# A router's maximum subtracted on VectorE: a transformer block with two-of-four experts on one Trainium2 core

## The chip, the core and the metric

The kernel runs on one core of one Trainium2 chip. A core has five engines that run side by side, each with its own queue of instructions that it takes strictly in order: TensorE (PE; its weight loads are shown apart as PEld), VectorE (DVE), ScalarE (ACT), GpSimd (POOL) and SyncE (SP), which issues most of the transfers. An instruction starts when its engine has reached it and the semaphores that it waits for have been raised. SBUF is the on-chip memory, 128 partitions wide; PSUM is the memory that TensorE writes to. "128x8" means 128 partitions of eight columns.

The metric is the device time of one execution in microseconds (us). A profile is one further execution, recorded by the hardware; its span is the time from its first to its last instruction.

## What is computed

32 sequences of 256 tokens with 128 channels pass through one pre-norm block: attention with 16 heads of 8 channels, in which the softmax is replaced by a rational function of the score minus the row's maximum, and a feed-forward layer of four experts, of which each token uses the two with the highest probability:

```python
x = x + attn(layernorm(x), w_qkv, w_out, b_out)
x = x + ffn(layernorm(x), router_w, router_b, w1, w3, w2)

# ffn, for all tokens xf (t, d)
logits = xf @ router_w + router_b                    # (t, 4)
probs = softmax(logits, axis=-1)
top_p, top_i = top_k(probs, 2)
top_p = top_p / sum(top_p, axis=-1)
gates = zeros((t, 4)); gates[token, top_i] += top_p
h = silu(einsum('td,edf->etf', xf, w1)) * einsum('td,edf->etf', xf, w3)
out = einsum('te,etd->td', gates, einsum('etf,efd->etd', h, w2))
```

Everything is float32. The softmax's common divisor drops out of the gates: it is enough to take exp(logit - maximum), set the two smaller ones to zero and divide by the sum of the rest.

## The kernel before

One sequence is one *block* b, 0 to 31. A block's 256 tokens lie on the 128 partitions in two halves, so that a tile with one number per token is 128x2, and the router's logits (four per token) are 128x8. The work of a block is cut into some sixty kinds of *steps*, each a small Python function that issues a few instructions on one engine (`ENGINE`, L73, says which). A planner (`plan`, L274) lays the steps of all blocks out in one order, by hand-set ranks (`RANK`, `OVER`), assumed costs (`COST`) and the numbers of buffers (`LIMIT`); `tile_block` then issues them in that order, and each engine's queue holds its share of it. A step's rank, its dependencies and its cost in the plan do not change when the body of its function does. The blocks overlap deeply: while ScalarE works at the attention of one block, TensorE runs the experts of an earlier one.

The steps that matter here, with their lines and the names that the profile shows:

- **Router.** `r_df` (GpSimd, L868 to L882) makes the logits `lg` from the normalised tokens, and `df`, 128x32, which says for each pair of experts which comes first; its last instruction is L882. `r_cnt` (VectorE) takes the maximum over the four logits of a token, negated, into `nm` (L888), and counts in `cnt` how many experts come ahead of each (L889). `r_exp` (ScalarE) takes the exponential in place, through the helper `act` (all its instructions have line L569): once for each half of the tokens, because a bias is one number per partition. `r_gs` (GpSimd) turns `cnt` into a mask (L900) and multiplies the exponentials by it (L901); `r_sm` (VectorE) sums them and takes the reciprocal (L905, L906); `r_ga` (GpSimd, L912) scales.
- **Tables.** ScalarE's functions come in tables. `act` loads a table where the function needs another than the last one (L567): one that holds the logarithm and the exponential serves `r_exp` and the attention's `l_ln` and `l_exp`; silu needs another. So there are two loads a block, and in most blocks one of them stands right behind `r_exp`.
- **Attention.** TensorE writes scores into two PSUM buffers, `ps_sc` (`c_pe`, L699: one buffer for scores to be processed, one for scores of a later block of which only the extreme is sought). VectorE's `x_red` reads the second (L710, `mt<-ps_sc`); ScalarE's `m_sq` squares the first (`dt<-ps_sc,sqb`), VectorE's `m_poly` completes it (L754, `dt<-dt,ps_sc`). TensorE's next scores into a buffer wait for L710 or L754. `l_prod` (L762) and `l_back` (L782) on GpSimd and `l_ln`, `l_exp` on ScalarE make reciprocals; `av` multiplies by the values.
- **After it.** `p_evac` and `tr_copy` are ScalarE's copies out of PSUM (`otsb`, `rxnT`, `ronT`, `rxn2T`); `p_norm` on VectorE divides (L812 and L814, `rc` and `on`); `p_add` makes the second norm's statistics (L835 to L845); `split` on GpSimd cuts float32 into two parts (L508, L509; `q<-qr` for queries and keys, `hxnT`, `lxnT` for tokens). In the first two blocks some of these splits run on VectorE.
- **Experts.** `u_a` and `u_b` on TensorE (`ps_ab<-hxn2T,w1h` and the like), `u_silu` on ScalarE (`sl<-ps_ab`), `u_mul` on VectorE (L940, `ht<-sl,ps_ab`), `d_pe` on TensorE (`ps_ab<-w2s,ht`), `d_acc` on VectorE (L956).

The queue on VectorE holds, in nearly all blocks, L888, L889 and then the next `x_red` or `m_poly`. On GpSimd the split of the queries and keys (L508, L509) follows directly on `r_df` in blocks 4 to 25.

Of the kernel before, what the change touches and what calls it, by code (L numbers as in the profile page):

```python
# [10 lines left out]
F32 = mybir.dt.float32  # L11
F32R = mybir.dt.float32r
I32 = mybir.dt.int32
AF = mybir.ActivationFunctionType
ALU = mybir.AluOpType
AX = mybir.AxisListType
# [4 lines left out]
E, FF = 4, 512  # L21
P = 128
# [53 lines left out]
    DVE="x_red x_fin m_poly p_norm p_add r_cnt r_sm u_mul d_acc ln1_stats setup_wqk setup_const",  # L76
# [379 lines left out]
def tile_block(ctx: ExitStack, tc: tile.TileContext, x, wqk, wv, wo, bo, rw, rb, w1, w3, w2, out):  # L456
    nc = tc.nc
    NB = x.shape[0]
    PE, ACT, DVE, POOL, SP = nc.tensor, nc.scalar, nc.vector, nc.gpsimd, nc.sync
# [33 lines left out]
    p2 = ctx.enter_context(tc.tile_pool(name="p2", bufs=2))  # L493
# [8 lines left out]
    st = {}  # L502
# [61 lines left out]
    def act(o, i, f, **kw):  # L564
        need = SET_SILU if f == AF.Silu else SET_LNEXP if f in (AF.Ln, AF.Exp) else None
        if need and cur["set"] != need:
            ACT.preload_act_table_set(need)  # L567
            cur["set"] = need
        ACT.activation(o, i, f, **kw)  # L569
# [314 lines left out]

    def r_cnt(b):
        lg, df = st["rt", b]
        nm, cnt = p2.tile([P, 2], F32, tag="nm", name="nm"), p2.tile([P, 2, E], F32, tag="cnt", name="cnt")
        DVE.tensor_reduce(nm, lg, axis=AX.X, op=ALU.max, negate=True)  # L888
        DVE.tensor_reduce(cnt, df, axis=AX.X, op=ALU.add)  # L889
        st["cnt", b] = cnt, nm  # L890

    def r_exp(b):
        pr, (_, nm) = st["rt", b][0], st["cnt", b]
        for c in range(2):
            act(pr[:, c], pr[:, c], AF.Exp, bias=nm[:, c : c + 1])

    def r_gs(b):
        pr, _ = st["rt", b]
        cnt, _ = st.pop(("cnt", b))
        POOL.tensor_scalar(cnt, cnt, 2.0, 1.0, ALU.is_lt, ALU.mult)  # L900
        POOL.tensor_tensor(pr, pr, cnt, op=ALU.mult)  # L901

# [188 lines left out]
```

## Time and profile before

| | |
|---|---|
| time, median of 3 runs | 1104.97 us (1104.2 to 1105.72) |
| the profiled execution: time | 1104.63 us |
| its span, first to last instruction | 1102.7 us |
| granted TensorE clock, mean | 0.961 (1.00 from 236.48 to 871.90 us) |
| busy: PE, DVE, ACT, POOL | 1046.3, 949.4, 938.6, 780.6 us |
| the two exponentials `lg<-lg,nm`, 128x4 each | 64 instructions, mean 348 ns |
| L888 and L889 | 32 of each, mean 146 and 181 ns |
| table loads L567 | 64, 1283 ns each |

A timeline's row gives the start (us from the span's beginning), the length, engine, line, operation, names (written from read), shapes, and in brackets the engine's idle time before it with what ended that. Rows of one engine may overlap a little: an instruction that waits for nothing starts before the end of its forerunner has been recorded. The chain of waits is found by going back from the last instruction, at each step to what released it; its pieces are the stretches that the end of the program hangs on. Idle time of an engine off that chain costs nothing. Busy time is an average over stages and says little of what a change is worth; a weight load or matmul that is held up may also count as busy. "Releasers" are inferred from semaphores, and of several the last one is named.

### The profile page before, as it was taken

To read this page: it belongs to the slowest core of one execution; us is meant where nothing else is said; L and a number is where in the kernel's file an instruction comes from. 1 tells how busy PE (TensorE), PEld (TensorE's weight loads), DVE (VectorE), ACT (ScalarE), POOL (GpSimd) and SP (SyncE) were. 2 spreads that over 40 slices of the span, in tenths; PEclk is the share of its full clock that TensorE was granted. 3 is DMA by queue.
4 is the path that set the end of the run, shared out by engine and by line. 5 is a ranking of instruction groups with operands and counts; after the bars stand their busy time and mean duration, and the time that the engine had idled before them with its cause. 6 is when DMAs were issued, how large, how long until landed. Compare 5 with 4: busy or idle time off the path is not lost.

```text
span 1102.7 us, 25445 instructions
## 1 busy us (share of the span) xinstructions
PE 1046.3 (95%) x10025; PEld 867.5 (79%) x10025; DVE 949.4 (86%) x1662; ACT 938.6 (85%) x1157; POOL 780.6 (71%) x1063
## 2 busy tenths in 40 slices
PE   4578999999999999999999999999999999999988
PEld 3345787888888888888888888888888888888878
DVE  5777899899899998899999998899998889898644
ACT  2388888889988888999888889988888999888962
POOL 3457787687787787887877787877877887756320
PEclk7557999999999999999999999999999999999999
DMA  4722012221112222211122122122222211220000
GB/s 145 252 70 89 23 59 73 92 75 62 46 46 94 76 74 69 94 52 47 61 75 95 68 76 75 37 69 73 75 74 69 75 47 42 72 74 9 6 5 11
DMA packets 51791, 75.11 MB, mean 68 GB/s; under 512 B 5080, under 2 KB 41432, under 8 KB 47704
## 3 DMA queue, kind: packets, MB, share of 16 engines
q1 hardware_dynamic: 50664, 72.24, 19.4%
q8 instruction: 79, 1.29, 0.5%
q10 hardware_dynamic: 1008, 1.25, 0.3%
q14 instruction: 40, 0.33, 0.1%
HBM read 42.27 MB, written 31.20 MB: 67 GB/s over the span
## 4 chain that ended last, share of the span: by engine, by line
ACT 55%; PE 32%; DVE 5%; issue 3%; POOL 2%; DMA 2%; ACTq 0%; DVEq 0%
ACT dt L569 31%; PE ps_ab L505 27%; ACT prod L569 9%; ACT L567 6%; PE ps_sc L505 4%; ACT sl L569 4%; POOL dt L782 2%; DVE mt L710 2%; DVE dt L754 2%; DVE ht L940 1%; ACT qr L627 1%; ACT lg L569 1%; ACT rxnT L597 1%; ACT rxn2T L597 1%; ACT va L642 1%
## 5 line engine op out<-in xcount | busy, mean ns | idle before, releaser
L710 DVE TENSOR_REDUCE mt<-ps_sc 128x4 f32<-128x1024 f32 x256 | 310.8, 1217 | 37.1 <-PE ps_sc L505 36.8
L754 DVE SCALAR_TENSOR_TENSOR dt<-dt,ps_sc 128x1024 f32<-128x1024 f32 x256 | 310.3, 1213 | 18.7 <-ACT dt L569 13.5
L569 ACT ACTIVATE dt<-ps_sc,sqb 128x1024 f32<-128x1024 f32 x256 | 286.2, 1120 | 32.8 <-PE ps_sc L505 32.6
L782 POOL TENSOR_TENSOR dt<-dt,prod 128x2048 f32<-128x2048 f32 x59 | 271.4, 4603 | 14.5 <-ACT prod L569 14.1
L505 PE MATMUL ps_ab<-w2s,ht 128*128 128x128 f32 x2048 | 263.8, 278 | 1.1 <-DVE ht L940 1.1
L569 ACT ACTIVATE dt<-dt 128x2048 f32<-128x2048 f32 x138 | 260.7, 1920 | 0.2 <-DVE dt L754 0.2
L505 PEld LDWEIGHTS ps_ab<-w2s,ht 128*128 128x128 f32 x2048 | 242.7, 192 | 16.6 <-issue 9.9
L569 ACT ACTIVATE sl<-ps_ab 128x512 f32<-128x512 f32 x256 | 149.7, 597 | 74.6 <-PE ps_ab L505 63.2
L762 POOL TENSOR_TENSOR prod<-dt 128x1024 f32<-128x1024 f32 x59 | 141.2, 2394 | 90.1 <-DVE dt L754 90.0
L940 DVE TENSOR_TENSOR ht<-sl,ps_ab 128x512 f32<-128x512 f32 x256 | 169.0, 680 | 28.7 <-PE ps_ab L505 20.6
L505 PE MATMUL ps_sc<-qk 26*128 26x256 f32 (+1 forms) x2048 | 159.4, 346 | 20.4 <-DVE dt L754 9.7
L505 PE MATMUL ps_ab<-hxn2T,w1h 128*128 128x256 f32 x512 | 159.8, 312 | 4.4 <-DVE ht L940 1.4
L505 PEld LDWEIGHTS ps_sc<-qk 26*128 26x128 f32 (+1 forms) x2048 | 98.2, 193 | 72.8 <-issue 18.1
L505 PE MATMUL ps_ab<-hxn2T,w3h 128*128 128x256 f32 x512 | 153.9, 301 | 0.0
L505 PE MATMUL ps_ab<-hxn2T,w1l 128*128 128x256 f32 x512 | 144.3, 282 | 0.0
L505 PE MATMUL ps_ab<-lxn2T,w3h 128*128 128x256 f32 x512 | 144.2, 282 | 0.0
L505 PE MATMUL ps_ab<-lxn2T,w1h 128*128 128x256 f32 x512 | 144.1, 281 | 0.0
L505 PE MATMUL ps_ab<-hxn2T,w3l 128*128 128x256 f32 x512 | 144.1, 281 | 0.0
L505 PE MATMUL ps_ab<-dt,va 128*32 128x256 f32 x2048 | 137.4, 399 | 7.0 <-ACT dt L569 3.7
L569 ACT ACTIVATE prod<-prod 128x1024 f32<-128x1024 f32 x118 | 125.0, 1060 | 0.8 <-POOL prod L762 0.4
L505 PEld LDWEIGHTS ps_ab<-hxn2T,w1h 128*128 128x128 f32 x512 | 96.4, 188 | 24.0 <-ACT sl L569 8.8
L505 PEld LDWEIGHTS ps_ab<-hxn2T,w3h 128*128 128x128 f32 x512 | 96.6, 189 | 8.4 <-issue 1.6
(124 smaller groups left out, 1558.4 us busy)
## 6 DMA issues: line engine op xcount, KB each, us to landing
qk<-scr SPq DMA_DIRECT2D x31, 1024.0 KB
scr<-q SPq DMA_DIRECT2D x125, 128.0 KB
scr<-q SPq DMA_DIRECT2D x29, 256.0 KB
out_dram<-x SPq DMA_DIRECT2D x32, 128.0 KB
xg<-in_x_dram SPq DMA_DIRECT2D x7, 512.0 KB
ws<-in_w_dram SPq DMA_DIRECT2D x8, 256.0 KB
qk<-scr SPq DMA_DIRECT2D x2, 512.0 KB
mscr<-m SPq DMA_DIRECT2D x31, 32.0 KB
```

Source lines behind the costliest of these rows:

```text
L505: PE.matmul(o, l, r, start=start, stop=stop, skip_group_check=True)
L567: ACT.preload_act_table_set(need)
L569: ACT.activation(o, i, f, **kw)
L597: ACT.copy(raw, st.pop((i, b)))
L627: ACT.copy(qr, st.pop(("qkP", b)))
L642: ACT.copy(v36[:, :, :, 26 * r : 26 * r + HD], pv[:, :, :D].rearrange("p c (a r d) -> p c a r d", r=2, d=HD)[:, :, :, r])
L710: DVE.tensor_reduce(o, st.pop(("xP", b, t)), axis=AX.X, op=ALU.min, negate=True)
L754: DVE.scalar_tensor_tensor(d, d, C, st.pop(("mP", b, s)).rearrange("p j c s -> p (j c s)"), ALU.add, ALU.mult)
L762: POOL.tensor_tensor(pr, d[:, :, 0], d[:, :, 1], op=ALU.mult)
L782: POOL.tensor_tensor(d, d, pr[:, :, None, :].to_broadcast([P, 4, 2, S]), op=ALU.mult)
L940: DVE.tensor_tensor(ht, st.pop(("sl", b, s)), st.pop(("uP", b, s, 1)), op=ALU.mult)
```

## The change

The maximum is kept as it is instead of negated, VectorE subtracts it from the logits in place, and ScalarE takes one exponential of all eight columns without a bias. The order of the steps stays, so the subtract stands in VectorE's queue right behind the count (L889), and the exponential where the two were.

```diff
     def r_cnt(b):
         lg, df = st["rt", b]
-        nm, cnt = p2.tile([P, 2], F32, tag="nm", name="nm"), p2.tile([P, 2, E], F32, tag="cnt", name="cnt")
-        DVE.tensor_reduce(nm, lg, axis=AX.X, op=ALU.max, negate=True)
+        mx, cnt = p2.tile([P, 2], F32, tag="mx", name="mx"), p2.tile([P, 2, E], F32, tag="cnt", name="cnt")
+        DVE.tensor_reduce(mx, lg, axis=AX.X, op=ALU.max)
         DVE.tensor_reduce(cnt, df, axis=AX.X, op=ALU.add)
-        st["cnt", b] = cnt, nm
+        DVE.tensor_tensor(lg, lg, mx[:, :, None].to_broadcast([P, 2, E]), op=ALU.subtract)
+        st["cnt", b] = cnt
 
     def r_exp(b):
-        pr, (_, nm) = st["rt", b][0], st["cnt", b]
-        for c in range(2):
-            act(pr[:, c], pr[:, c], AF.Exp, bias=nm[:, c : c + 1])
+        pr = st["rt", b][0]
+        act(pr, pr, AF.Exp)
 
     def r_gs(b):
         pr, _ = st["rt", b]
-        cnt, _ = st.pop(("cnt", b))
+        cnt = st.pop(("cnt", b))
         POOL.tensor_scalar(cnt, cnt, 2.0, 1.0, ALU.is_lt, ALU.mult)
         POOL.tensor_tensor(pr, pr, cnt, op=ALU.mult)
```

In the instruction lists of the two programs VectorE has 32 instructions more, each behind L889 and waiting for VectorE's own L888; ScalarE has 32 activations less; the lists of TensorE and GpSimd are the same. The exponential waits, as before, for VectorE and GpSimd.

## The prediction, made before the changed kernel ran

> **What bounds the kernel now.** I read the chain of waits first, then engine timelines around one block of the even middle stretch (blocks 4 to 24 repeat every 31.76 us). The page's chain by engine:
>
> ```profile
> ACT 55%; PE 32%; DVE 5%; issue 3%; POOL 2%; DMA 2%; ACTq 0%; DVEq 0%
> ```
>
> The same chain in order of time (start, us, what), around the exponential of block 13:
>
> ```profile
> 521.69 0.45 ACT rxnT L597
> 522.14 0.38 ACT lg L569 x2
> ...
> 522.53 1.28 ACT L567
> 523.82 0.01 issue
> 523.83 0.61 ACT sl L569
> ...
> 524.48 3.83 PE ps_ab L505 x30
> ```
>
> ScalarE (ACT) is never idle from 533.28 of one block to 522.5 of the next; the two exponentials (`lg L569 x2`) stand in that run, before a table load (L567) and the first silu, whose end lets TensorE go on. From 524.48 TensorE has the chain until the last silu (533.88). So ScalarE time saved at the exponential counts in full, if no other path reaches 524.48 first.
>
> **What is removed.** Two ACTIVATEs of 128x4 with a bias per partition (64 in all, mean 348 ns) become one of 128x8 without. In the chain the old pair occupies 0.38 us; mid-stream they follow each other, and the next one them, by 0.188 each, again 0.376. The new one is not in the trace. From above: it behaves as one of the old, 0.19. From below: an eight-column copy (`xb L644`) takes 0.06 of the chain. Nearest are Exp without bias, from SBUF: 2048 columns 1.92 us, 1024 columns 1.06, so 0.84 ns a column; two in a row of 2048 take
>
> ```profile
> 513.46 3.73 ACT L569 ACTIVATE dt<-dt 128x2048 f32<-128x2048 f32 x2
> ```
>
> so the second adds 1.81, that is 0.09 beyond its columns (2048 x 0.84 = 1.72). I take 0.09 + 8 x 0.00084 = 0.10 for the new one: 0.38 - 0.10, rounded down, is **0.27 us a block** (bounds 0.19 to 0.32).
>
> Does 524.48 follow? Before it TensorE's last weight load of `ident,on` started 0.486 earlier; where it needn't wait (blocks 1 and 3) the next follows by 0.115, so 0.37 is free. VectorE (DVE) must start `ht` (L940) too; its row follows `sm L906` by 0.276, and rows that wait for nothing follow L906 by 0.083, so 0.19 is free there. It then runs back to back until its `dt L754` releases the scores that TensorE starts at 528.24: L754 ends 0.131 before, while in a case where TensorE really waited for L754 (539.78) it took 0.05, so 0.08 more is free. 0.19 + 0.08 = 0.27: the whole saving just fits. VectorE's rows (start, us):
>
> ```profile
> 519.97 0.13 DVE L888 TENSOR_REDUCE nm<-lg 128x2 f32<-128x8 f32 x1
> 520.01 0.17 DVE L889 TENSOR_REDUCE cnt<-df 128x8 f32<-128x32 f32 x1
> 520.11 1.21 DVE L710 TENSOR_REDUCE mt<-ps_sc 128x4 f32<-128x1024 f32 x1
> 521.42 1.22 DVE L754 SCALAR_TENSOR_TENSOR dt<-dt,ps_sc 128x1024 f32<-128x1024 f32 x1
> 522.89 0.36 DVE L812 RECIPROCAL rc<-ps_m 128x32 f32<-128x32 f32 x1 [0.24 <-PE ps_m L806]
> ...
> 524.18 0.17 DVE L906 RECIPROCAL sm<-sm 128x2 f32<-128x2 f32 x1
> ```
>
> **What is added.** One TENSOR_TENSOR of 128x8 on VectorE between L889 and whatever follows. Not in the trace; `ht` (512 columns, 0.68) and `on` (256, 0.424) give 1.0 ns a column and 0.17 fixed, so 0.18 alone; L710 starts 0.09 after L889 does, so in the queue it costs about 0.1. The maximum without negation stays the same row (L888).
>
> ScalarE's exponential now waits for the subtract, behind L889, instead of L888. In blocks 4 to 24 the exponential starts 1.76 to 1.94 after L889 ends, so 0.1 to 0.5 more hides behind ScalarE's own queue. Only blocks 27, 28 and 29 have just 0.09 to 0.15; behind the exponential there stand the table load and the silus.
>
> But the subtract reads two SBUF tensors while GpSimd (POOL) is at work. Two spots of the trace show VectorE and GpSimd shutting each other out. GpSimd first, VectorE made to wait to its end: L844, 128x2, 0.17 us in each other block, here took 1.48, ending with GpSimd's L762 at 182.14:
>
> ```profile
> 180.69 1.48 DVE L844 TENSOR_SCALAR ve<-mv 128x2 f32<-128x2 f32 x1
> ```
> ```profile
> 179.75 2.39 POOL L762 TENSOR_TENSOR prod<-dt 128x1024 f32<-128x1024 f32 x1
> ```
>
> VectorE first, in a TENSOR_TENSOR of two SBUF tensors, and GpSimd's L577 (0.45 elsewhere) stretched to 0.91:
>
> ```profile
> 12.90 0.69 DVE L509 TENSOR_TENSOR q<-qr,q 128x512 fp32r<-128x512 f32 x1
> ```
> ```profile
> 13.00 0.91 POOL L577 TENSOR_SCALAR xn<-xg,y,nb 128x128 f32<-128x128 f32 x1
> ```
>
> Not every operation does so: L906 runs inside GpSimd's L577 in all of blocks 4 to 22 at an even 0.166. So the subtract's wait lies between nothing and the whole rest of GpSimd's instruction; since the second pair is of its own form, I take the whole rest, ending 0.03 after GpSimd's, as L844 did.
>
> A page of the Trainium skill, "SBUF — State Buffer" (section "Who interferes with whom"), says this of the form: a VectorE instruction with both inputs in SBUF and a GpSimd instruction that reads SBUF exclude each other, and the later waits out the earlier. It speaks against the change; by it the sum is the one with the waits, without it the first rival's.
>
> Where does the subtract land? In blocks 4 to 25 always inside GpSimd's L508, which stands in its queue right behind the `df` that L889 needs:
>
> ```profile
> 519.90 0.62 POOL L508 TENSOR_SCALAR q<-qr 128x512 fp32r<-128x512 f32 x1
> 520.60 1.29 POOL L509 TENSOR_TENSOR q<-qr,q 128x512 fp32r<-128x512 f32 x1
> ```
>
> It ends at 520.55. L710 then starts at 520.47 (rows here start 0.08 before their forerunner's end), 0.36 late; L754 1.13 later, at 521.60, 0.18 late, since it had waited 0.10 for ScalarE anyway; L812 could start 1.14 after that, at 522.74, and has to wait for TensorE until 522.89. **Nothing is lost, with 0.15 to spare**; what hides the subtract are VectorE's waits before L754 and L812. (The scores at 523.49 start 0.85 after L754's end.) In block 25 these waits are missing: L754 to L906 come 0.4 late, eat the 0.37 of TensorE's slack, and the saving is gone.
>
> In blocks 2 and 3 the subtract would start at 155.99 and 189.22, inside
>
> ```profile
> 154.63 4.61 POOL L782 TENSOR_TENSOR dt<-dt,prod 128x2048 f32<-128x2048 f32 x1 [1.19 <-ACT prod L569]
> ...
> 188.89 4.58 POOL L782 TENSOR_TENSOR dt<-dt,prod 128x2048 f32<-128x2048 f32 x1 [2.19 <-ACT prod L569]
> ```
>
> (answers of two windows). Block 2: free at 159.27, L710 at 159.2 instead of 156.0, L754 at 160.33 instead of 157.29, over at 161.55. TensorE's next scores need that L754 (they are in hand at 158.5 now): done 162.1, and ScalarE's square, 159.88 now, starts at 162.15: **2.3 us**, in a stretch that is ScalarE's chain without a gap. Block 3: free at 193.50, L754 from 191.56 to 194.55, over at 195.77, scores done 196.3, the square from 194.15 to 196.35: **2.2 us**. Block 29's exponential (1027.66) would wait for GpSimd's L585 (until 1028.13): its successor comes 0.27 late instead of 0.27 early.
>
> **Sum.** Savings: 21 blocks (4 to 24) x 0.27 = 5.67; blocks 2, 3 and 30, also on the chain, 0.81; block 27 0.2; block 29 -0.27; blocks 0, 1, 26, 28, 31 nothing (TensorE or VectorE has the chain); block 25 nothing: 6.4 us. Losses 2.3 + 2.2 = 4.5. Net -1.9 against the profiled execution's 1104.63 us (span 1102.7 and 1.9 outside). That execution lies 0.34 below the median of 1104.97, so **1103.1 us**. Own range: a saving of 0.2 to 0.29 a block gives 4.8 to 6.9; losses of 3.5 to 5.3, as the L754 of those blocks is late by less or more; 1101.5 to 1105.5.
>
> **Rivals.**
> 1. *No waiting for GpSimd.* For: L906 doesn't wait, and at 8.21 a TENSOR_TENSOR of two SBUF tensors (0.60 instead of 0.42) ended before GpSimd's L540 (7.51 to 8.94) did. Against: L844, and the pair at 12.90. The losses vanish, blocks 25 and 29 save too: 5.67 + 0.81 + 0.2 + 2 x 0.27 = 7.2, 1097.8 us.
> 2. *The saving is smaller.* The new exponential occupies ScalarE like one of the old (0.19), or the path over VectorE, whose slack fits the saving only just, gives 0.19 a block. Then 21 x 0.19 + 3 x 0.19 + 0.1 - 0.35 = 4.3, eaten by the 4.5: 1105.2 us, no change.
> 3. *VectorE loses to L509 as well.* If GpSimd's L509, 0.08 behind L508, goes ahead of the waiting subtract, this ends at 521.92, not 520.55. The 0.15 to spare is the point from which it decides: L812 comes 1.2 late, `on` and with it TensorE's 524.48 over 0.8 late even with a faster exponential, and the `ht` behind it 1.0. 22 blocks x 1.0 + 4.5 = +26: 1131 us. Against: L509 needs L508's result and starts only 0.08 after it, while the subtract stands ready.
>
> **How the numbers follow.** A difference of 0.2% (2.2 us) is about what a measurement of this kernel can tell from none, so faster means below 1102.8, slower above 1107.2. Forecast 0.58 (0.25 of it below 1102.8, 0.31 within, 0.02 above), rival 1 0.15, rival 2 0.17, rival 3 0.10. Faster 0.25 + 0.15 = 0.40; same 0.31 + 0.17 = 0.48; slower 0.12. The range 1098.5 to 1105.8 leaves out rival 3 and the greater part of rival 1.
>
> **What would show it.** A single exponential row near 0.2 us, and the table load starting 0.27 sooner after `rxnT`. A subtract row of 0.18 us in blocks 26 to 28, but near 0.45 in the even stretch and of 3 to 4 us in blocks 2 and 3, each ending with GpSimd's instruction; ScalarE waiting about 2 us before a square (`dt<-ps_sc,sqb`) in blocks 2 and 3. A period of 31.49 instead of 31.76 us. Subtracts of 0.18 everywhere would make rival 1 right; a period still above 31.6, rival 2; subtracts of 1.8, rival 3.

## The result: slightly slower, and where the time went

| | before | after |
|---|---|---|
| time, median of 11 runs | 1105.03 us (1104.2 to 1105.93) | 1107.5 us (1105.83 to 1108.5) |
| ratio to before, 95% interval | | 1.0022 (1.0013 to 1.0032) |
| profiled execution: time, span | 1104.63, 1102.7 us | 1108.5, 1106.6 us |

The kernel became 2.5 us slower where 1.9 us less were forecast. The new rows come first: three groups of the maximum, the subtract and the exponential in the changed kernel (count, then shortest, median and longest duration in ns, first and last start in us).

```profile
L888 DVE TENSOR_REDUCE mx<-lg x32: 128/152/162, 93.5 to 1078.0; 128x2 f32<-128x8 f32 x32
L890 DVE TENSOR_TENSOR lg<-lg,mx x32: 156/432/4230, 95.2 to 1079.8; 128x8 f32<-128x8 f32 x32
L569 ACT ACTIVATE lg<-lg x32: 192/293/302, 96.1 to 1081.8; 128x8 f32<-128x8 f32 x32
```

One exponential stands where two stood. The subtract takes anything from 0.16 to 4.23 us for the same eight columns. Two of the 32 are long: 3.20 us in block 2 and 4.23 us in block 3. The one in block 2 ran from 155.89 to 159.09, and on GpSimd this instruction ran beside it:

```profile
154.51 4.55 POOL L782 TENSOR_TENSOR dt<-dt,prod 128x2048 f32<-128x2048 f32 x1 [1.19 <-ACT prod L569]
```

The even stretch looks otherwise; VectorE's timeline of the changed kernel around block 13:

```profile
527.28 0.13 DVE L888 TENSOR_REDUCE mx<-lg 128x2 f32<-128x8 f32 x1
527.33 0.18 DVE L889 TENSOR_REDUCE cnt<-df 128x8 f32<-128x32 f32 x1
527.45 0.37 DVE L890 TENSOR_TENSOR lg<-lg,mx 128x8 f32<-128x8 f32 x1
527.74 1.21 DVE L710 TENSOR_REDUCE mt<-ps_sc 128x4 f32<-128x1024 f32 x1
528.88 1.20 DVE L754 SCALAR_TENSOR_TENSOR dt<-dt,ps_sc 128x1024 f32<-128x1024 f32 x1
530.20 0.36 DVE L812 RECIPROCAL rc<-ps_m 128x32 f32<-128x32 f32 x1
```

The subtract ends at 527.82, as GpSimd's L508 (527.19, 0.62 long) does; nothing behind it is late enough to matter. The table load after the exponential, which in the profile of before came every 31.77 us, now comes every 31.52: 0.25 us gained in each block. Within the block it starts 0.58 us after `rxnT` instead of 0.85, the 0.27 that the prediction named as a sign. Against the profile of before that table load is 9.07 us late in block 4, 4.32 in block 24 (one delay of 0.4 between blocks 7 and 8 included) and 3.66 in block 31. So the whole loss lies ahead of block 4: the squares there are 9.4 us later than the first ones were. The chain of waits of the changed kernel shows how it began, around block 2 (start, us, what):

```profile
155.95 3.14 DVE lg L890
159.09 1.13 DVE mt L710
160.22 1.14 DVE dt L754
161.36 0.04 issue
161.41 0.50 PE ps_sc L505 x5
161.91 6.10 PE ps_ab L505 x38
168.01 0.44 PE ps_sc L505 x8
```

Up to the scores (`ps_sc`) at 161.41 this is the prediction's own path. After that TensorE (PE) holds the chain for 6.1 us with 38 matmuls, and no step of the prediction spoke of those. ScalarE's rows of the same stretch:

```profile
161.85 1.11 ACT L569 ACTIVATE dt<-ps_sc,sqb 128x1024 f32<-128x1024 f32 x1 [1.96 <-PE ps_sc L505]
162.86 3.81 ACT L569 ACTIVATE dt<-dt 128x2048 f32<-128x2048 f32 x2
168.48 1.12 ACT L569 ACTIVATE dt<-ps_sc,sqb 128x1024 f32<-128x1024 f32 x1 [1.81 <-PE ps_sc L505]
```

It waits twice: 1.96 us before the square that was foreseen, and 1.81 more before the next one, 6.6 us later. In the profile of before these squares started at 159.88 and 164.48, with no wait:

```profile
159.88 1.13 ACT L569 ACTIVATE dt<-ps_sc,sqb 128x1024 f32<-128x1024 f32 x1
...
164.48 1.13 ACT L569 ACTIVATE dt<-ps_sc,sqb 128x1024 f32<-128x1024 f32 x1
```

Block 3 repeats it: squares late by 2.28, then by 2.40 and 0.94 more. The windows of the changed kernel say why; these are cut where the granted clock changes, each 3.41 us long. (Columns: from and to, length, busy time and instructions of each engine, granted TensorE clock PEclk, DMA share, GB/s.)

```profile
155.11:158.53 3.42, 2.93 (x26) 2.61 (x26) 3.42 (x6) 3.42 (x5) 3.42 (x1) 1.00 0.05 14
158.53:161.94 3.41, 0.92 (x9) 0.58 (x9) 3.41 (x6) 1.45 (x2) 3.33 (x4) 1.00 0.00 0
161.94:165.35 3.41, 3.41 (x17) 3.41 (x18) 2.79 (x3) 3.41 (x3) 3.04 (x2) 0.50 0.00 0
...
196.08:199.49 3.41, 0.38 (x2) 0.18 (x2) 3.41 (x4) 1.90 (x2) 3.33 (x4) 1.00 0.00 0
199.49:202.91 3.42, 3.41 (x26) 1.91 (x27) 3.42 (x6) 2.77 (x2) 3.42 (x2) 0.50 0.02 5
202.91:206.32 3.41, 3.41 (x18) 3.41 (x18) 0.92 (x3) 2.15 (x3) 1.43 (x6) 0.50 0.00 0
```

While VectorE (third busy time) stood in the subtract, TensorE (first) ran out of matmuls: 0.92 us busy out of 3.41 in block 2, 0.38 in block 3. In the windows that follow, the granted clock is 0.50, for one window in block 2 and for two in block 3. In the profile of before the clock is 1.00 all through this stretch and TensorE is busy, as a window of that profile shows:

```profile
158.50:162.00 3.50, 3.50 (x34) 3.30 (x33) 3.22 (x6) 3.50 (x3) 3.42 (x4) 1.00 0.00 0
```

The 24 weight loads of `w2s` that follow the scores took 4.38 us at the half clock, against 2.76 before (the changed kernel first):

```profile
161.84 4.38 PEld L505 LDWEIGHTS ps_ab<-w2s,ht 128*128 128x128 f32 x24
```
```profile
159.00 2.76 PEld L505 LDWEIGHTS ps_ab<-w2s,ht 128*128 128x128 f32 x24
```

So the suspicion after one profile is: half of the loss is the wait of the subtract, the other half a slower TensorE that this wait brings about.

Two lines of the changed kernel's profile page, the clock by slices and the chain by engine:

```profile
PEclk7557999899999999999999999999999999999999
...
PE 70%; ACT 14%; DVE 6%; POOL 5%; issue 2%; DMA 2%; ACTq 0%; DVEq 0%; POOLq 0%
```

The 8 in the eighth slice (from 193.7 us) is block 3's half clock. The chain, ScalarE's for 55% before, is TensorE's for 70% now, most likely since the even stretch now hangs on TensorE's path, which the prediction had at 0.27 us behind ScalarE's: of the first two experiments below, the one that changes the even stretch alone has PE at 56%, the one that leaves it has ACT at 52%.

### The profile page after: what moved, and what is told of

Its sections match the earlier page's. It is cut to its first block, busy times and chain, and to the rows that moved or that the text cites. A ratio compares the mean times of both kernels' runs of the same rounds, so it can differ in the third digit from the quotient of the medians.

```text
span 1106.6 us, 25444 instructions
## 1 busy us (share of the span) xinstructions
PE 1046.2 (95%) x10025; PEld 871.9 (79%) x10025; DVE 959.8 (87%) x1694; ACT 931.8 (84%) x1125; POOL 780.3 (71%) x1063
## 4 chain that ended last, share of the span: by engine, by line
PE 70%; ACT 14%; DVE 6%; POOL 5%; issue 2%; DMA 2%; ACTq 0%; DVEq 0%; POOLq 0%
PE ps_ab L505 55%; PE ps_sc L505 9%; ACT dt L569 9%; POOL dt L782 4%; PE ps_m L592 3%; ACT prod L569 2%; DVE mt L710 2%; PE ps_m L505 2%; PE ps_m L806 2%; DVE dt L754 2%; ACT L567 1%; ACT sl L569 1%; DVE lg L890 1%; DVE ht L940 1%; DMA scr<-q 1%
## 5 line engine op out<-in xcount | busy, mean ns | idle before, releaser
L710 DVE TENSOR_REDUCE mt<-ps_sc 128x4 f32<-128x1024 f32 x256 | 310.7, 1216 | 37.2 <-PE ps_sc L505 36.9
L782 POOL TENSOR_TENSOR dt<-dt,prod 128x2048 f32<-128x2048 f32 x59 | 270.2, 4583 | 14.3 <-ACT prod L569 14.0
L505 PE MATMUL ps_ab<-w2s,ht 128*128 128x128 f32 x2048 | 267.3, 281 | 1.1 <-DVE ht L940 1.1
L505 PEld LDWEIGHTS ps_ab<-w2s,ht 128*128 128x128 f32 x2048 | 246.3, 194 | 17.1 <-issue 10.7
```

What stands on the lines that cost most here:

```text
L505: PE.matmul(o, l, r, start=start, stop=stop, skip_group_check=True)
L710: DVE.tensor_reduce(o, st.pop(("xP", b, t)), axis=AX.X, op=ALU.min, negate=True)
L782: POOL.tensor_tensor(d, d, pr[:, :, None, :].to_broadcast([P, 4, 2, S]), op=ALU.mult)
```

## The experiments

The theory after this result, A: the subtract waits for GpSimd's running instruction; in blocks 2 and 3 that leaves TensorE without work, and its clock halves; the even stretch gains as forecast. Rivals: the loss comes from elsewhere; only operations with two SBUF tensors wait; the second half of the loss is work that queued up, whatever the clock.

**Where the loss and the gain sit.** Blocks 2 and 3 keep the old form, all others the new one; and the reverse. In both:

```diff
+        if NEW(b):
             DVE.tensor_tensor(lg, lg, mx[:, :, None].to_broadcast([P, 2, E]), op=ALU.subtract)
```

with `NEW` true for all blocks but 2 and 3, or for these alone; where it is false, the maximum is negated and two exponentials with a bias are taken as before.

> Blocks 2 and 3 keep the negated maximum and the two exponentials with a bias; the other 30 blocks have the change. Theory A (the whole loss of the changed kernel comes from the two subtracts that wait behind GpSimd's L782, 3.2 and 4.2 us, and from what TensorE loses after them; elsewhere the change gains 0.25 us a block): no subtract row over 0.8 us, the stretch up to block 4 as before, 1098 to 1100 us. Rival B (the subtract or the later exponential costs something in every block): 1103 us or more. Rival C (TensorE's half clock at 162 and 199 us came by chance): the half clock appears here too and 3 to 4 us of the loss stay, 1102 to 1104 us.

Measured: 1098.79 us (1098.07 to 1099.37), ratio 0.9944 (0.9932 to 0.9957). The longest of its subtracts took 0.73 us, and the clock stayed full from 102.70 to 1048.19 us: rivals B and C don't fit.

> Only blocks 2 and 3 have the change, the other 30 are as before. Theory A: the same two waits of 3.2 and 4.2 us, the same stalls of ScalarE's squares behind them, a half clock of TensorE near 162 and 200 us, and no gain elsewhere: 1105 + 9 = 1112 to 1115 us. Rival B: 1104 to 1107 us, since two blocks of 32 cost a sixteenth of little. Rival C: the waits cost 4 to 6 us, 1109 to 1111 us, without a half clock.

Measured: 1114.27 us (1112.71 to 1114.52), ratio 1.0081 (1.0067 to 1.0095). Its two subtracts took 3.19 and 4.24 us, the half clock came at 161.4 and 198.95, and the squares jumped by 2.07 and 2.01 in block 2, by 2.28, 2.34 and 0.94 in block 3. (A jump is what a square's lateness against the profile of before grows by from the square ahead of it.) So the two edits are separate: against the 1104.81 us of before on that chip, 30 blocks gain 6.0 and two blocks lose 9.5. The sum, 3.5, is 1.0 more than the 2.5 of the changed kernel; each of the two intervals is some 1.4 us wide to either side.

**What the exponential alone is worth.** No maximum, no subtract, one exponential of the plain logits.

```diff
-        DVE.tensor_reduce(mx, lg, axis=AX.X, op=ALU.max)
         DVE.tensor_reduce(cnt, df, axis=AX.X, op=ALU.add)
-        DVE.tensor_tensor(lg, lg, mx[:, :, None].to_broadcast([P, 2, E]), op=ALU.subtract)
```

> The maximum and its subtract are left out in all blocks; one exponential of the plain logits (the gates are a ratio, so the subtrahend drops out as long as nothing overflows). Theory A: 21 blocks gain 0.25, a period of 31.5 us, blocks 2 and 3 gain 0.27 each instead of losing, 25 and 29 gain too: 1097 to 1099 us, within 2 us of the kernel that keeps blocks 2 and 3. Rival B (a subtract costs in every block): a period below 31.35 us and 1094 us or less.

Measured: 1097.14 us (1096.87 to 1097.41), ratio 0.9929 (0.9915 to 0.9942), with 0.26 us gained in each block. Leaving the subtract out altogether gives hardly more in the even stretch than the subtract that waits (0.25): there it is hidden.

**Is it the form of the instruction?** The subtract as two operations of one SBUF tensor each, with the maximum as a scalar per partition.

```diff
-        DVE.tensor_tensor(lg, lg, mx[:, :, None].to_broadcast([P, 2, E]), op=ALU.subtract)
+        for c in range(2):
+            DVE.tensor_scalar(lg[:, c], lg[:, c], mx[:, c : c + 1], 1.0, ALU.subtract, ALU.mult)
```

> The subtract is made of two TENSOR_SCALARs of 128x4 with the maximum as a scalar per partition, so that only one SBUF tensor is read. If only an operation with two SBUF tensors is shut out by GpSimd, they take 0.17 us each everywhere and the time is 1098 to 1101 us. If it is as with L844 (one SBUF tensor, and it waited), the first of them waits in blocks 2 and 3 for 3 to 4 us and in the even stretch for 0.3 to 0.5 us: 1106 to 1110 us.

Measured: 1109.63 us (1108.14 to 1112.81), ratio 1.0046 (1.0029 to 1.0063). The group of these instructions, the pair in block 2, and the GpSimd instruction beside it (from three views of this kernel's trace, the times again start and length):

```profile
L891 DVE TENSOR_SCALAR lg<-lg,mx x64: 216/224/4239, 95.6 to 1084.2; 128x4 f32<-128x4 f32 x64
```
```profile
158.96 3.58 DVE L891 TENSOR_SCALAR lg<-lg,mx 128x4 f32<-128x4 f32 x2
```
```profile
157.58 4.56 POOL L782 TENSOR_TENSOR dt<-dt,prod 128x2048 f32<-128x2048 f32 x1 [1.19 <-ACT prod L569]
```

The first of the pair took 3.20 us and ended 0.02 after L782 did (162.14); the longest, 4.24 us, is the first of block 3's. So it isn't the two SBUF tensors of a TENSOR_TENSOR alone: a TENSOR_SCALAR waits in the same way, as L844 did in the profile of before. The Trainium skill's page "SBUF — State Buffer", section "Who interferes with whom", counts `tensor_scalar` among the operations that can enter a two-port mode and then exclude GpSimd. The waits agree with it; that these instructions ran in that mode no run here shows. On TENSOR_REDUCE, which the page says never contends on this chip, the changed kernel's trace agrees too: L888 started inside L782 in block 2 (155.72) and took 0.14 us. (In the profiled execution of the pair, the slowest of its four, the half clock came at 99.78 and 130.50 us as well, before block 2.)

**Is lateness of VectorE enough?** The kernel without subtract, with VectorE held in block 2 by reductions of a resident tensor, which wait for nobody; their result isn't used. First 2048 and 700 columns (3.2 us), then 1300 columns once (1.5 us).

```diff
         DVE.tensor_reduce(cnt, df, axis=AX.X, op=ALU.add)
+        if b == 2:
+            for n in (2048, 700):
+                DVE.tensor_reduce(dmy, w2s.rearrange("p e c d -> p (e c d)")[:, :n], axis=AX.X, op=ALU.add)
```

> As the kernel without maximum and subtract, but in block 2 VectorE reads a constant tile behind the count for about 3 us (two TENSOR_REDUCEs of 2048 and 700 columns, one SBUF tensor): VectorE is late as with the blocked subtract, and nothing is shut out. If only VectorE's lateness counts, block 2 loses what it lost in the changed kernel, 2.0 us at the square near 160 and 2.0 at the next, with a half clock of TensorE near 161: 1097.1 + 3.9 = 1101 us. If the shut-out did more than make VectorE late (GpSimd slower too), less than half of that: below 1099.3 us.

Measured: 1101.67 us (1099.14 to 1103.31), ratio 0.9968 (0.9957 to 0.9979): 4.5 us more than without the delay by the medians, 4.3 by the ratios. The squares jumped by 2.03 and 1.94, as in the changed kernel.

> The same with one TENSOR_REDUCE of 1300 columns, about 1.5 us. By the lateness alone, reckoned as in the prediction, the square near 160 comes 0.5 us late. If a half clock follows only on a longer idle time of TensorE, that is all: 1097.5 to 1098.0 us and no half clock near 161. If every idle time brings it, 1.5 us more: 1099 to 1100 us.

Measured: 1097.26 us (1096.9 to 1098.25), ratio 0.9935 (0.9921 to 0.9948): 0.1 us more than without the delay by the medians, 0.7 by the ratios, less than the intervals can tell. The windows of the two, long delay first:

```profile
160.55:163.96 3.41, 0.74 (x8) 0.38 (x8) 3.39 (x5) 1.79 (x1) 3.33 (x4) 1.00 0.04 10
163.96:167.38 3.42, 3.42 (x20) 3.19 (x17) 3.13 (x5) 3.13 (x3) 3.42 (x2) 0.50 0.00 0
```
```profile
157.65:161.06 3.41, 2.44 (x23) 1.92 (x22) 3.41 (x6) 3.25 (x4) 3.33 (x4) 1.00 0.01 3
161.06:164.48 3.42, 3.42 (x35) 3.30 (x33) 2.29 (x4) 3.42 (x3) 3.42 (x1) 1.00 0.00 0
```

So the cost needs no wait for GpSimd: a VectorE that is late for another reason is enough. A delay of 3.2 us leaves TensorE 0.74 us of work in a window and costs 4.3 to 4.5 us; half the delay leaves 2.44 us and costs 0.1 to 0.7. The price does not rise evenly with the delay. (In the profiled execution with the long delay the half clock showed up at 99.1 and 129.8 us as well, before block 2. That the runs of this kernel spread over 4 us may come from there; the difference of the medians is therefore less sure than the 3.97 us of the two jumps.)

**Is the second half the clock or the queue?** The changed kernel with TensorE given useless work in the two gaps: an expert product behind the held scores (`d_pe`, second half of the first expert, of blocks 1 and 2) is computed several times over, each time from the start, so that its result stays. The first try repeated it six and seven times more.

```diff
-        for fc in range(4):
+        for fc in [k for _ in range(1 + {(1, 3): 6, (2, 3): 7}.get((b, i), 0)) for k in range(4)]:
```

> The changed kernel; in front of the held scores of blocks 2 and 3 TensorE repeats the four matmuls of the down projection that stands there 6 and 7 times (the same result each time), 2.8 and 3.3 us of work in its idle time. If the second half of the loss is the half clock that follows on TensorE's idle time, there is no half clock near 161 and 199, the first late squares stay 2 us late, the later ones lose little, and the time falls by about 5 us to 1102 to 1103.5 us. If it is the work queued up behind the held scores, the half clock is gone all the same, but the time stays at 1106 to 1108.5 us.

Measured: 1108.98 us (1108.35 to 1109.66), ratio 1.004 (1.0027 to 1.0052). This one missed by its own size: one repeat is eight matmuls, not four, and the filler took 5.4 and 6.3 us instead of 2.8 and 3.3 (the weight loads of `w2s` at the two spots took 7.23 us each, against 1.87 and 0.97 without it). The clock stayed full from 92.5 to 1058 us, but now the first square came 4.32 us late because of the filler itself, and the second only 0.3 more. It decides nothing on the time. The same with three repeats more at both spots, beside the changed kernel on one chip:

> The changed kernel, but the expert products d_pe of block 1 and of block 2 (second half of the first expert) are computed four times over instead of once, 24 more TensorE matmuls at each of the two spots, some 2.85 us at the full clock, which fit into the 3.1 and 3.3 to 3.7 us that TensorE stood idle behind the held scores; each repeat starts its sum anew, so the output stays. Theory A (the second half of the loss is the halved clock that follows TensorE's idle time): no window of half clock between 100 and 1050 us, block 2 loses 2.0 to 2.6 us in all instead of 4.1 and block 3 2.3 to 3.2 instead of 5.6, so 1102.0 to 1104.0 us. Theory B (the second half is the work that queued up behind the held scores, whatever the clock): the clock stays full, but the second jumps of the squares remain, 1106 to 1108.5 us. If the half clock stays although TensorE is kept busy, A's cause is wrong.

Measured: 1104.2 us (1103.49 to 1105.2), ratio to before 0.9994 (0.9985 to 1.0003).

> The changed kernel again, on the same chip as the run with three repeats: both theories 1106.5 to 1108.5 us, with half-clock windows near 162 and 199 us.

Measured: 1107.47 us (1106.29 to 1109.77), ratio 1.0026 (1.0017 to 1.0035). The windows around both spots, with the filler first, then without:

```profile
158.37:161.79 3.42, 3.30 (x29) 2.98 (x28) 3.42 (x4) 1.94 (x2) 3.34 (x4) 1.00 0.00 0
161.79:165.20 3.41, 3.35 (x32) 3.21 (x33) 3.41 (x7) 2.90 (x2) 3.41 (x2) 1.00 0.02 5
195.92:199.33 3.41, 2.65 (x30) 2.09 (x32) 3.41 (x7) 1.42 (x2) 3.33 (x4) 1.00 0.00 0
199.33:202.75 3.42, 3.42 (x39) 2.91 (x28) 3.42 (x6) 2.83 (x3) 3.16 (x5) 1.00 0.00 0
```
```profile
159.97:163.39 3.42, 1.90 (x17) 1.56 (x18) 3.42 (x6) 1.46 (x3) 3.40 (x2) 1.00 0.00 0
163.39:166.80 3.41, 3.41 (x18) 3.41 (x17) 2.40 (x4) 3.41 (x3) 2.06 (x2) 0.50 0.00 0
...
197.52:200.93 3.41, 1.18 (x16) 0.75 (x20) 3.41 (x6) 1.45 (x3) 3.33 (x4) 1.00 0.00 0
200.93:204.35 3.42, 3.42 (x26) 2.46 (x18) 3.01 (x4) 2.82 (x3) 3.23 (x5) 0.50 0.02 5
```

48 matmuls more, whose results change nothing, make the kernel 3.3 us faster (1107.47 to 1104.2). ScalarE's two squares of block 2 in the kernel with the filler:

```profile
162.30 1.11 ACT L569 ACTIVATE dt<-ps_sc,sqb 128x1024 f32<-128x1024 f32 x1 [1.99 <-PE ps_sc L505]
163.31 3.81 ACT L569 ACTIVATE dt<-dt 128x2048 f32<-128x2048 f32 x2
167.31 1.12 ACT L569 ACTIVATE dt<-ps_sc,sqb 128x1024 f32<-128x1024 f32 x1 [0.18 <-PE ps_sc L505]
```

The first wait is what it was (1.99 us); the second has shrunk from 1.81 to 0.18. The jumps are 2.11 and 0.41 in block 2 and 2.11 and 0.45 in block 3, 5.1 us in all. Without the filler the run beside it had 4.12 and 4.28 us, 8.4 in all; the 3.3 between them is the difference in time. So the second half is the clock, but for the 0.41 and 0.45 that stay of it. The median lies 0.2 above A's range; in the profiled execution a half window at 127.7 us, ahead of both spots, had cost 0.8, which may be why.

**Without the wait.** The subtract of blocks 2 and 3 on GpSimd, where it stands behind L782 in the queue.

```diff
-        DVE.tensor_tensor(lg, lg, mx[:, :, None].to_broadcast([P, 2, E]), op=ALU.subtract)
+        (POOL if b in (2, 3) else DVE).tensor_tensor(lg, lg, mx[:, :, None].to_broadcast([P, 2, E]), op=ALU.subtract)
```

> The changed kernel, but in blocks 2 and 3 the subtract runs on GpSimd, in whose queue it stands right behind L782; the exponential there has 6 and 5 us to spare. If the waits of these two blocks are all that the change loses, 1098.0 to 1099.3 us, level with the kernel that keeps the two exponentials there. If GpSimd's 0.2 us in front of its splits count, 1 us more.

Measured: 1098.05 us (1097.54 to 1101.26), ratio 0.9946 (0.9933 to 0.9958). GpSimd's rows of block 2:

```profile
154.58 4.58 POOL L782 TENSOR_TENSOR dt<-dt,prod 128x2048 f32<-128x2048 f32 x1 [1.21 <-ACT prod L569]
159.10 0.22 POOL L890 TENSOR_TENSOR lg<-lg,mx 128x8 f32<-128x8 f32 x1
```

The subtract is done at 159.32, hardly later than VectorE had it (159.09), but VectorE goes on with L710 at 155.94, and TensorE's clock stays full. This version, which leaves nothing out, beats both kernels: 6.6 us less than before by the medians (1104.67 on that chip), 6.0 by the ratio.

## Why the prediction was wrong

- **The wait of the subtract: right.** It was put at "the whole rest" of GpSimd's instruction: measured 3.20 us in block 2 and 4.23 in block 3, each to the end of L782 (159.07 and 197.16) plus 0.02. "No waiting for GpSimd" (rival 1) is refuted; its 1097.8 us is near what came where the wait was taken away (1097.14 and 1098.05). What spoke for it stays unexplained: the TENSOR_TENSOR at 8.21 ended inside GpSimd's L540, so not every instruction of GpSimd holds VectorE to its end.
- **The saving: right.** 0.27 us a block was forecast, 0.25 came, 0.26 without any subtract, and 0.27 where GpSimd took the subtracts of blocks 2 and 3. Where blocks 2 and 3 keep the old form, the sum leaves 6.4 - 2 x 0.27 = 5.9 us to be gained; 6.0 came. The exponential's row is 0.19 to 0.23 us long outside the even stretch, near the forecast "0.2"; in blocks 4 to 24 it is 0.29 to 0.30. Rival 2 (0.19 a block) falls.
- **The even stretch: right.** The subtract took 0.30 to 0.47 us there (0.20 in block 4) and ended with L508, so L509 didn't go ahead of it: rival 3 falls. "Nothing is lost, with 0.15 to spare" held within 0.02 a block.
- **The tail: small misses.** Block 29 lost 0.31 us (forecast 0.27), block 30 gained 0.27 (0.27); block 25 gained 0.28 where nothing was forecast, blocks 26 and 31 0.13 and 0.27 likewise, and block 27 nothing where 0.2 was. Blocks 25 to 31 gained 0.65 together instead of 0.2.
- **Two readings were slightly off, with no effect on the sum.** L906 stands inside L577 in blocks 4 to 22 except block 6, and the exponential starts 1.76 to 1.89 us after L889 ends in blocks 4 to 24; the 1.94 is block 31's.
- **The step that failed: "2.3 us" for block 2 and "2.2 us" for block 3.** The mechanism was right and the term of the sum too small: 4.1 us in block 2 (2.08 + 2.03) and 5.6 in block 3 (2.28 + 2.40 + 0.94) in the profiled execution, 9.7 together, where the working allowed "losses of 3.5 to 5.3". The first squares came 2.08 and 2.28 late, as forecast. The working followed the delay to ScalarE's first late square and stopped there. It didn't ask what TensorE does while VectorE holds the scores: it runs out of work, and its next 3.4 to 6.8 us are granted half the clock, a cost that the sum left out. With TensorE kept busy the loss is 5.1 us in the trace, close to the 4.5 of the sum.

With the measured 9.7 in place of 4.5, the sum gives 1104.63 - 6.4 + 9.7 = 1107.9 us; the profiled execution took 1108.5, the median is 1107.5. (The savings in that profile add up to 6.0 instead of 6.4.)

## What to carry to other kernels

An instruction of eight columns on VectorE can wait for nearly the whole of the GpSimd instruction beside it (4.23 of 4.56 us here; a TENSOR_REDUCE did not), so look up what GpSimd runs at that moment in each block that differs from the even stretch, and put such a step on GpSimd itself where it queues behind that instruction anyway. When a delay is followed through the profile, follow it on every engine that is fed through it, TensorE above all: where it had been without work for 1.5 to 3 us of a window of 3.4 us at blocks 2 and 3, the half clock followed, and in block 2 the delay was paid twice. A short delay can be nearly free where one twice as long costs more than itself.

## What the runs showed of the hardware

- **The half clock comes in whole windows on a fixed grid.** In each profile the changes of clock lie a multiple of 3.41 us apart. Of the windows at blocks 2 and 3, those in which TensorE was busy for 0.38 to 1.90 us of 3.41 were followed by the half clock; those with 1.99 us (with the pair of TENSOR_SCALARs, from 198.77), 2.17 us (the changed kernel beside the filler, from 156.56), 2.44 us and more were not. That is no limit that holds elsewhere: with the long delay, the half clock followed windows with 2.39 us (from 95.70) and 2.12 us (from 126.42), with three repeats one with 2.24 us (from 124.25); with the subtract on GpSimd it did not follow one with 1.71 us (from 1045.78). At blocks 2 and 3 it lasted two windows after 0.38 and 0.49 us and one after 0.74 us and more, but at the end of the profile of before it lasted one after 0.43 us (from 1050.43). The page "TensorE: Matmul & The Clock Gate" of the Trainium skill, section "What's actually happening", tells of a free-running window of 3413 ns, which agrees, and puts the half clock behind a window that was idle. Here no window was idle throughout, and up to 1.90 us of matmuls in it didn't keep the clock. The longest stretch without a weight load in the changed kernel was 2.22 us in block 2 and 2.68 in block 3. What decides, no run here settles; the busy share of one window alone doesn't.
- **The same idle stretch costs differently by how the grid cuts it.** Block 3's, with 2.68 and 0.94 us without a weight load in both profiles of the changed kernel, was followed by two half windows in the first and by one in the second, and the second jump was 2.40 us in the one and 1.23 in the other.
